# A gated cross-attention and local-attention block on one core: another table of piece times

## The chip, the core and the metric

The kernel runs on one core of one Trainium2 chip. A core has TensorE (matrix products and transposes; PE in the profile, PEld for its weight loads), VectorE (DVE), ScalarE (ACT), GpSimd (POOL) and the DMA queues, among them SP's. Each engine works through its own queue of instructions in order, and engines wait for each other by semaphores. The metric is the time of one execution on the device, in microseconds, lower is better; it is a median over runs.

## The reference

Eight sequences of 256 positions and 128 features go through a gated cross-attention (16 heads of 8) to a context of the same size, and then through six layers. Each layer is a local attention (16 heads of 64, windows of 32 that also see the window before) and a feed-forward with GELU. Half of the features are shifted by one position ahead of each. All is float32.

```python
x = x + tanh(g_xattn[0]) * xattn(layernorm(x), ctx, ctx, Wq, bq, Wk, bk, Wv, bv, Wo, bo)
x = x + tanh(g_ffn[0]) * ffn(layernorm(x), Wqkv, q_scale, k_scale, Wo, ln_g, ln_b, W1, b1, W2, b2)

# ffn: for each of 6 layers
x = attn_layer(shift_tokens(x), Wqkv[i], q_scale[i], k_scale[i], Wo[i]) + x
x = ffn_layer(shift_tokens(x), ln_g[i], ln_b[i], W1[i], b1[i], W2[i], b2[i]) + x

# attn_layer: q, k, v = split(x @ Wqkv); q, k = l2norm(q) * qs, l2norm(k) * ksc
#   rotary embedding with a scale; softmax of 8 * q k^T in windows, masked; times v; @ Wo
# ffn_layer: xn = norm(x) * g + bln; a, gate = split(xn @ W1 + b1); (a * gelu(gate)) @ W2 + b2
```

## The kernel before

A unit of work is one sequence in one layer, so there are 48 of them (`sequence(k, l, b, ...)`, k = 8 l + b), and eight cross-attentions ahead (`cross(b)`). Each is cut into named pieces; a piece is a function that issues a few instructions to one engine. For a unit the pieces are, in the order of the data:

- `proj`cx (TensorE, L537): projection of chunk c, half x, full width 128 x 128, 512 columns. Chunks 0 to 3 are keys and queries of the first 128 positions, then of the second. `sq`cx (ScalarE, L545) squares it, `rot`cx (VectorE, L553) multiplies it by the rotary tables, `ss`c (VectorE, L562) sums the squares, `radd`c (GpSimd, L568) adds the rotated halves.
- `norms` (ScalarE), `ninv` (VectorE, L584), `nrm`c (GpSimd, L591): the norms, applied. `pqt`c (TensorE, L601): transposes of 64 x 128; `qe`cx (ScalarE, L609) copies them out of PSUM. `vp`tx and `ve`tx: the values, like a projection (L616, L624).
- `sc`ti (TensorE, L637): scores of position tile t, head group i, small products of 64 x 32. `mx`gi (VectorE, L653): mask and maximum; `ex`gi (ScalarE, L663): exponentials; `rs`g (VectorE, L672), `div`g (GpSimd, L678).
- `pt`t (TensorE, L696): transposes of the probabilities, 32 x 64 and 32 x 128; `pe`tx (L705, L707) copies them out, on VectorE but for `pe00` on ScalarE; `co` (VectorE, L713) adds a corner.
- `at`c and `aw`c (TensorE, L734): attention times values in 64 x 64 pieces, in two phases, with `av`c (VectorE, L745) between; `oe`c (ScalarE, L748); `wo`x (TensorE, L757): the output projection; `oadd` (VectorE).
- `ftr` (TensorE, L770), `fst` (VectorE, L187 to L190), `frs` (GpSimd, L194), `fno` (VectorE, L198), `fba` (TensorE, L786), `faf` (VectorE, L791), `fga` and `fva` (TensorE, L806), `fge` (ScalarE, L813), `fgt` (VectorE, L819), `fdo` (TensorE, L830), `fad` (VectorE): the feed-forward.

A float32 product is two passes, and each pass is a weight load and a matmul; a transpose is one pass. So `sc`, `pt` have 128 TensorE instructions each, `at` and `aw` 64, `pqt` 32, `wo` 16, `fga`, `fva`, `fdo` 12, and `proj`, `vp`, `ftr`, `fba` 4.

The order is written out by hand. `PLAN` gives each piece a time in slots, a unit begins every 5 slots, and all pieces of all units are issued in the order of these times; only the order counts:

```python
    def at(k, piece, fn, *args):
        time = PLAN[piece] if isinstance(piece, str) else piece
        pieces.append((k * SLOTS + time, len(pieces), fn, args))
    ...
    with tc.manual_schedule():
        for _, _, fn, args in sorted(pieces, key=lambda p: p[:2]):
            fn(*args)
```

The times run to 22 slots, so at any moment four or five units are under way. `CROSS_SHIFT` moves the cross-attentions, and `LOAD_...` the weight loads on SP.

PSUM is held in three pools of two banks or bank pairs, which new tiles take in turn; a tile waits until the one two before it in its pool has been read. `ps_p` holds `proj`, `vp` and `ftr` (tags `pj`, `pv`, `px`), `ps_s` bank pairs for `pqt`, `sc` (both halves of a t in one tile), `pt`, `at` and `fga`, and `ps_m` single banks for `pt` (two), `wo`, `fba`, `fva` and `fdo`:

```python
    ps_p = ctx.enter_context(tc.tile_pool(name="ps_p", bufs=2, space=PSUM))
    ps_s = ctx.enter_context(tc.tile_pool(name="ps_s", bufs=2, space=PSUM))
    ps_m = ctx.enter_context(tc.tile_pool(name="ps_m", bufs=2, space=PSUM))
```

Of the kernel before, what the change touches and what calls it, by code (L numbers as in the profile page):

```python
# [34 lines left out]


PLAN = {
    "proj01": 0.00028, "sq01": 0.24563, "rot01": 0.27022, "proj00": 0.28172, "sq00": 0.47163,
    "rot00": 0.62148, "proj11": 0.99963, "ss0": 1.00345, "sq11": 1.0853, "rot11": 1.30237,
    "proj10": 1.30872, "sq10": 1.4114, "rot10": 1.47598, "ss1": 1.73479, "proj21": 2.11884,  # L40
    "radd1": 2.17109, "proj20": 2.19741, "sq21": 2.23333, "sq20": 2.26223, "rot21": 2.32903,
    "rot20": 2.35456, "ss2": 2.50695, "proj31": 2.58908, "radd2": 2.94111, "sq31": 2.95069,
    "rot31": 3.0918, "radd0": 3.47769, "proj30": 4.10239, "sq30": 4.10778, "rot30": 4.76634,
    "ss3": 4.85725, "norms": 5.18912, "radd3": 5.5946, "ninv": 5.62034, "nrm1": 5.71832,
    "nrm2": 6.19927, "pqt2": 6.5031, "vp00": 6.57359, "ve00": 6.87853, "nrm0": 7.09745,
    "nrm3": 7.10145, "qe21": 7.17779, "qe20": 7.24908, "pqt1": 7.30269, "pqt0": 7.30815,
    "qe11": 7.79232, "qe10": 7.79416, "qe01": 7.86086, "qe00": 7.86486, "sc01": 8.08564,
    "sc00": 8.08586, "mx01": 8.33529, "mx00": 8.575, "mx10": 8.73408, "ex01": 8.84437,
    "mx11": 9.0029, "pqt3": 9.30081, "qe30": 9.30558, "vp11": 9.34495, "qe31": 9.3858,
    "ve11": 9.41571, "ex00": 10.61127, "sc10": 10.70937, "sc11": 10.76862, "mx20": 11.07451,  # L50
    "mx30": 11.14518, "mx21": 11.1494, "ex10": 11.20658, "ex11": 11.25952, "mx31": 11.27208,
    "rs1": 11.44471, "ex30": 12.07331, "rs0": 12.16906, "ex31": 12.50422, "rs3": 12.72523,
    "div1": 12.89348, "div0": 12.89748, "pt0": 12.97352, "ex20": 13.08661, "pe01": 13.22005,
    "vp10": 13.2685, "pe00": 13.59856, "ex21": 13.65127, "ve10": 13.68936, "div3": 13.87906,
    "rs2": 14.07853, "div2": 14.3002, "pe02": 14.40755, "pt1": 14.70408, "co": 14.83618,
    "vp01": 14.9316, "pe12": 15.00601, "ve01": 15.15777, "pe11": 15.19144, "pe10": 15.19544,
    "at0": 15.39314, "av0": 15.52724, "aw0": 15.8366, "oe0": 15.91741, "at1": 16.24107,
    "av1": 16.25403, "aw1": 16.39146, "oe1": 16.45257, "wo0": 16.74993, "wo1": 17.29053,
    "oadd": 17.36809, "ftr": 17.79008, "fst": 17.79331, "frs": 17.9642, "fno": 18.23053,
    "fba": 18.70684, "faf": 19.0069, "fga": 19.48595, "fge": 19.57067, "fva": 20.02293,  # L60
    "fgt": 20.20234, "fdo": 21.23637, "fad": 21.58213, "zt": 21.88299, "zg": 21.95977,
    "xld": -23.23124, "xst": -22.91456, "xrs": -21.60601, "xno": -21.52631, "xt": -20.76317,
    "xte": -20.68889, "xqk": -19.98066, "xqe": -19.80688, "xke": -19.77245, "xb": -19.4014,
    "xs2": -18.39415, "xm22": -18.25296, "xm21": -18.24521, "xm20": -18.09159, "xvp": -18.05114,
    "xs1": -17.99064, "xve": -17.92105, "xm11": -17.83494, "xm12": -17.81429, "xm10": -17.72349,
    "xs0": -17.53644, "xm01": -17.50591, "xm02": -17.49705, "xm00": -17.31438, "xs3": -17.29615,
    "xm30": -16.85925, "xm31": -16.81729, "xm32": -16.77595, "xnt": -16.75807, "xnc": -16.74335,
    "xp1": -16.63391, "xe12": -16.58507, "xe11": -16.55896, "xe10": -16.41137, "xp0": -16.31426,
    "xa1": -16.29716, "xe02": -16.16779, "xe01": -16.16379, "xe00": -15.89622, "xo1": -15.86388,
    "xp3": -15.86254, "xa0": -15.77129, "xe31": -15.69042, "xe32": -15.66181, "xo0": -15.58029,  # L70
    "xe30": -15.44397, "xp2": -15.24929, "xa3": -15.19602, "xo3": -15.12433, "xe21": -15.10125,
    "xe22": -15.01431, "xe20": -14.75037, "xa2": -14.54131, "xo2": -14.30214, "xu0": -14.06924,
    "xd0": -14.0369, "xu1": -13.82959, "xd1": -13.5642, "xw": -13.34873, "xc": -13.29663,
    "xwo": -13.24607, "xx": -13.03102, "xst2": -12.64937, "xr2": -12.31015, "xn2": -11.66727,
    "xt2": -11.54082, "xsp": -11.45376,
}

CROSS_SHIFT = [0.0000000, -1.4843600, -2.9659400, -4.3950700, -5.7931900, -7.2641000, -8.5043100, -8.5733000]
LOAD_FIRST, LOAD_AFTER, LOAD_AFTER_CROSS = -19.7106000, 21.63, -19.98

P_ON_SCALAR = {(0, 0)}

# [2 lines left out]
def tile_gated_block(ctx: ExitStack, tc: tile.TileContext, a: dict, out: bass.AP):  # L85
# [117 lines left out]
    def cross(b):  # L203
# [203 lines left out]

        kx = b + CROSS_SHIFT[b] / SLOTS
        for n, fn in (
# [584 lines left out]
```

## Time and profile before

| | us |
|---|---|
| median of 3 runs (1817.76 to 1828.15) | 1821.45 |
| the profiled execution | 1818.11 |
| its span, first to last instruction | 1816.3 |
| busy: TensorE, VectorE, ScalarE, GpSimd | 1710.5, 1520.0, 1496.5, 1094.1 |
| first 166.8 us (cross-attention, no unit begun): TensorE busy | 149.7 |
| 460.1 to 1702.4 (units 8 to 46): TensorE busy of 1242.3 | 1202.0 |
| from the first projection of the last unit to the end | 113.9 |
| mean granted TensorE clock | 0.988 |

In a profile line of instruction groups the columns are the line of the kernel, the engine, the operation, the tiles (out<-in), the shapes and the count, then busy time and the mean duration of one in ns, and the idle time of the engine ahead of them with who ended it. "issue" as a releaser is time in which the engine waited for nothing that the profile shows. Matmuls are pipelined, so successive durations overlap; what a piece adds is the time from the end of the piece before it to its own end.

### The profile page before, as it was taken

The numbers are of one execution on the slowest core, as the hardware profiler recorded it, in microseconds if no ns is written. First come the engines' busy times: TensorE is split into PE (matmuls) and PEld (weight loads), VectorE is DVE, ScalarE is ACT, GpSimd is POOL, SyncE is SP. The second block draws the span as 40 slices with busy tenths as digits, with TensorE's granted clock in tenths as the row PEclk, the third lists the DMA queues.
The fourth block names the chain that finished last, engine by engine and source line by source line (L and its number), as shares of the span: only waits on it lengthen the run. The fifth ranks groups of instructions, "written<-read, shape, count | busy, mean of one in ns | idle before, by whom it ended". The sixth has DMA issues, their size and how long they took to land.

```text
span 1816.3 us, 78103 instructions
## 1 busy us (share of the span) xinstructions
PE 1710.5 (94%) x32948; PEld 1136.4 (63%) x32948; DVE 1520.0 (84%) x5314; ACT 1496.5 (82%) x4692; POOL 1094.1 (60%) x716
## 2 busy tenths in 40 slices
PE   7998888999999999999999999999999999999987
PEld 4565545666666666666666666666666666666664
DVE  3546667998988988899899989999899999998864
ACT  2343558998998988899989999999999999988883
POOL 3121346667676666766767676676767676766641
PEclk9999999999999999999999999999999999999998
DMA  3000002000010000010000010000100000000000
GB/s 94 7 13 11 3 2 68 3 4 3 3 48 22 3 3 3 3 49 22 3 3 3 22 49 3 3 3 3 49 22 3 3 3 4 3 6 6 8 7 10
DMA packets 34717, 26.33 MB, mean 14 GB/s; under 512 B 16058, under 2 KB 31294, under 8 KB 34366
## 3 DMA queue, kind: packets, MB, share of 16 engines
q1 hardware_dynamic: 33214, 21.20, 4.0%
q8 instruction: 259, 4.24, 1.0%
q14 instruction: 92, 0.75, 0.1%
q10 hardware_dynamic: 1152, 0.14, 0.0%
HBM read 20.28 MB, written 1.05 MB: 12 GB/s over the span
## 4 chain that ended last, share of the span: by engine, by line
PE 83%; DVE 9%; issue 5%; ACT 3%; POOL 0%; POOLq 0%; DVEq 0%; ACTq 0%
PE pj L537 18%; PE pv L616 11%; PE m L757 8%; PE po L734 8%; PE s L637 7%; PE pqt L601 6%; PE ppt L696 5%; PE s L806 5%; PE pssT L322 4%; DVE x_max L302 3%; PE pw L830 3%; PE pa L806 2%; DVE ur L553 2%; PE pox L340 1%; PE pssx L292 1%
## 5 line engine op out<-in xcount | busy, mean ns | idle before, releaser
L568 POOL TENSOR_TENSOR u<-ur 128x1024 f32<-128x1024 f32 x192 | 454.0, 2366 | 137.8 <-PE pqt L601 75.9
L663 ACT ACTIVATE pr<-pr,nmax 128x64 f32<-128x64 f32 x1536 | 513.5, 340 | 2.0 <-DVE nmax L653 1.4
L591 POOL TENSOR_TENSOR u<-u,rn 128x1024 f32<-128x1024 f32 x192 | 359.3, 1902 | 243.9 <-DVE rn L584 243.9
L537 PE MATMUL pj<-w_qkv,st 128*128 128x512 f32 x768 | 404.6, 619 | 7.0 <-DVE ur L553 3.6
L553 DVE TENSOR_TENSOR ur<-pj,rotk 128x1024 f32<-128x1024 f32 x192 | 227.1, 1203 | 85.2 <-ACT sq L545 85.2
L663 ACT ACTIVATION_READ_ACCUMULATOR pr<-pr,nmax 128x1 f32 x1536 | 294.8, 192 | 0.0
L545 ACT ACTIVATE sq<-pj 128x512 f32<-128x512 f32 x384 | 227.6, 593 | 56.8 <-PE pj L537 46.6
L678 POOL TENSOR_TENSOR pr<-pr,rs 128x512 f32<-128x512 f32 x192 | 198.6, 1046 | 91.8 <-DVE rs L672 91.8
L653 DVE CUSTOM_DVE_ANT_0 pr<-s,mask 128x64 f32<-128x64 f32 x1536 | 232.6, 219 | 17.3 <-PE s L637 16.7
L553 DVE TENSOR_TENSOR ur<-pj,rotq 128x1024 f32<-128x1024 f32 x192 | 232.7, 1212 | 15.4 <-ACT sq L545 14.3
L562 DVE TENSOR_REDUCE squares<-sq 128x16 f32<-128x1024 f32 x192 | 233.5, 1216 | 2.7
L616 PE MATMUL pv<-w_qkv,st 128*128 128x512 f32 x384 | 221.5, 659 | 1.3 <-DVE ur L553 1.0
L734 PEld LDWEIGHTS po<-prT,v 64*64 64x64 f32 x6144 | 134.3, 133 | 100.8 <-DVE nmax L653 33.4
L637 PE MATMUL s<-kT,qT 64*32 64x64 f32 x12288 | 151.9, 226 | 44.5 <-issue 44.5
L757 PEld LDWEIGHTS m<-oT,w_o 128*128 128x128 f32 x768 | 145.5, 190 | 58.9 <-issue 43.5
L757 PE MATMUL m<-oT,w_o 128*128 128x256 f32 x768 | 181.9, 380 | 0.0
L537 PEld LDWEIGHTS pj<-w_qkv,st 128*128 128x128 f32 x768 | 131.3, 192 | 79.9 <-issue 39.6
L734 PE MATMUL po<-prT,v 64*64 64x96 f32 (+1 forms) x6144 | 171.5, 243 | 8.9 <-issue 6.9
L624 ACT COPY v<-pv 128x512 f32<-128x512 f32 x192 | 112.7, 587 | 68.3 <-PE pv L616 68.2
L637 PEld LDWEIGHTS s<-kT,qT 64*32 64x32 f32 x12288 | 130.2, 105 | 58.7 <-issue 50.9
L194 POOL TENSOR_TENSOR rstd<-rstd,half_neg 128x2 f32<-128x2 f32 x64 | 45.0, 703 | 200.9 <-DVE rstd L190 173.1
L601 PEld LDWEIGHTS pqt<-ident,u 64*128 64x128 f32 x3072 | 106.7, 139 | 60.2 <-ACT pr L663 28.8
(116 smaller groups left out, 2863.3 us busy)
## 6 DMA issues: line engine op xcount, KB each, us to landing
w_qkv<-in_L_ffn_Wqkv SPq DMA_DIRECT2D x18, 512.0 KB, 6.1
w_o<-in_L_ffn_Wo SPq DMA_DIRECT2D x6, 512.0 KB, 4.0
w<-in_L_ffn_W SPq DMA_DIRECT2D x6, 341.0 KB, 2.9
xin<-in_x SPq DMA_DIRECT2D x8, 128.0 KB, 3.6
cin<-in_ctx SPq DMA_DIRECT2D x8, 128.0 KB, 2.1
out<-res SPq DMA_DIRECT2D x8, 128.0 KB, 1.8
w<-in_L_ffn_W SPq DMA_DIRECT2D x12, 64.0 KB, 3.5
rotq<-in_c_cos_q SPq DMA_DIRECT2D x6, 64.0 KB, 3.4
```

What stands on the lines that cost most here:

```text
L537: nc.tensor.matmul(pj, st[b][:, t * P : (t + 1) * P], w["qkv"][:, o : o + 512], start=True, stop=True,)
L545: nc.scalar.activation(sq[:, hs, :], c_["pj", c, half], AF.Square)
L553: nc.vector.tensor_tensor(ur[:, :, half * 512 : (half + 1) * 512].rearrange("p x (h d) -> p x h d", d=DH), pj.unsqueeze(1).to_broadcast([P ...
L562: nc.vector.tensor_reduce(squares[k % 2][:, t, i, :, 0], c_.pop(("sq", c)), AX.X, ALU.add)
L568: nc.gpsimd.tensor_tensor(u.rearrange("p h (two d) -> p h two d", two=2), ur[:, 0], ur[:, 1, :, ::-1, :], ALU.add,)
L591: nc.gpsimd.tensor_tensor(u, u, rn, ALU.mult)
L616: nc.tensor.matmul(pj, st[b][:, t * P : (t + 1) * P], w["qkv"][:, o : o + 512], start=True, stop=True,)
L637: nc.tensor.matmul(pss[n * WIN : (n + 1) * WIN, par, c, :], c_["qT"][rows, c, o : o + WIN], c_["kT"][rows, c, k0 : k0 + KEYS], start=True, ...
L653: nc.vector.tensor_tensor_reduce(probabilities(t)[:, par * NPAIR + c, :], c_["pss", t][:, par, c, :], mask[:, t, :], -1.0, 3e38, ALU.add, ...
L663: nc.scalar.activation(pr[:, col, :], pr[:, col, :], AF.Exp, bias=c_.pop(("nmax", g, c)), scale=-1.0, accum_out=c_["sums", t][:, col : col ...
L734: nc.tensor.matmul(po[par * DH : (par + 1) * DH, x, i, q0:q1], v[rows, t, h * DH : (h + 1) * DH], prT[rows, column[h], 64 * half : 64 * ha ...
L757: nc.tensor.matmul(pm, weights[l]["o"][:, c, :], oT[:, c, :], start=(first and c == 4 * half), stop=(not first and c == 4 * half + 3),)
```

## The change

The table is replaced: nearly every piece has another time, the cross-attentions another spacing, and the loads another place. No piece changes its instructions or its engine.

```diff
 PLAN = {
-    "proj01": 0.00028, "sq01": 0.24563, "rot01": 0.27022, "proj00": 0.28172, "sq00": 0.47163,
...
-    "qe11": 7.79232, "qe10": 7.79416, "qe01": 7.86086, "qe00": 7.86486, "sc01": 8.08564,
-    "sc00": 8.08586, "mx01": 8.33529, "mx00": 8.575, "mx10": 8.73408, "ex01": 8.84437,
...
-    "ve11": 9.41571, "ex00": 10.61127, "sc10": 10.70937, "sc11": 10.76862, "mx20": 11.07451,
...
+    "proj01": 0.0006328, "sq01": 0.1713858, "proj00": 0.1917734, "rot01": 0.2531156,
...
+    "radd0": 1.8177464, "rot20": 2.0866573, "proj21": 2.4116597, "sq21": 2.4285819,
+    "rot21": 2.8389973, "ss2": 3.0299221, "radd2": 3.4720543, "proj31": 3.6577322,
...
+    "pqt2": 8.1557951, "qe20": 8.3157299, "qe21": 8.3161644, "sc00": 8.5039716, "mx00": 8.7122873,
+    "pqt3": 8.9079072, "qe31": 8.9144684, "sc01": 8.920431, "mx10": 9.1908941, "qe30": 9.3090241,
...
+    "ex01": 10.2226495, "ex11": 10.4676246, "ex10": 10.6814012, "sc10": 10.7294329,
+    "mx30": 10.7734771, "mx20": 10.9018842, "rs1": 10.9979902, "sc11": 11.1160587,
...
 }
-CROSS_SHIFT = [0.0000000, -1.4843600, -2.9659400, -4.3950700, -5.7931900, -7.2641000, -8.5043100, -8.5733000]
-LOAD_FIRST, LOAD_AFTER, LOAD_AFTER_CROSS = -19.7106000, 21.63, -19.98
+CROSS_SHIFT = [0.0000000, -1.8673571, -3.6163960, -4.9323222, -6.8028984, -8.5383167, -10.3450958, -11.8335433]
+LOAD_FIRST, LOAD_AFTER, LOAD_AFTER_CROSS = -17.1923263, 20.96, -18.88
```

Sorted modulo 5 slots, the tables give the order of each engine's queue in the steady state. TensorE's, over one period (pieces of four or five units):

- before: `proj01 fva proj00 at0 sc10 sc11 aw0 proj11 fdo at1 proj10 aw1 pqt2 vp00 wo0 proj21 proj20 wo1 pqt1 pqt0 proj31 ftr pt0 sc01 sc00 vp10 fba proj30 pqt3 vp11 fga pt1 vp01`
- after: `proj01 fva proj00 at0 at1 aw0 fdo proj10 aw1 sc10 proj11 wo0 sc11 pqt1 vp00 proj20 wo1 proj21 pqt0 ftr pt0 vp10 pqt2 sc00 proj31 fba pqt3 sc01 proj30 vp11 fga pt1 vp01`

VectorE's, over the same:

- before: `pe12 pe11 pe10 fgt rot01 av0 ninv rot00 ss0 mx20 mx30 mx21 av1 mx31 rot11 rs1 rot10 fad ss1 rs0 rot21 rot20 oadd ss2 rs3 fst rot31 pe01 fno mx01 mx00 mx10 mx11 faf rs2 pe02 rot30 co ss3`
- after: `pe12 pe10 pe11 fgt av0 rot01 av1 rot00 ss0 ninv mx30 mx20 fad rot10 rs1 rot11 ss1 rs0 mx31 mx21 rot20 oadd rs2 rot21 fst pe02 ss2 fno mx00 pe01 faf rot31 mx10 rs3 mx11 mx01 rot30 co ss3`

## Prediction

> **What bounds the kernel now.** I read the page first, then who waited for whom, the DMA view, the chain in order of time over one period, and last the timelines of a period in which nothing stalls. The page:
>
> ```profile
> PE 1710.5 (94%) x32948; PEld 1136.4 (63%) x32948; DVE 1520.0 (84%) x5314; ACT 1496.5 (82%) x4692; POOL 1094.1 (60%) x716
> ...
> PE 83%; DVE 9%; issue 5%; ACT 3%; POOL 0%; POOLq 0%; DVEq 0%; ACTq 0%
> ```
>
> TensorE carries the chain, and 5% of it is "issue", time in which it waited for nothing that the profile shows. The waits say where:
>
> ```profile
> PEld s L637 <- issue: 50.9, 39, 2.0
> PE s L637 <- issue: 44.5, 37, 1.8
> ```
>
> These are the score products (both rows see the same gaps), about one gap of 1.2 us in each of the 48 periods. In the chain over 900 to 906 us one stands in the middle of the scores, right behind the transposes of probabilities:
>
> ```profile
> 901.49 1.13 PE ppt L696 x49
> 902.62 0.98 PE s L637 x65
> 903.60 1.19 issue
> 904.80 0.69 PE s L637 x44
> ```
>
> The DMA view gives the cause:
>
> ```profile
> q8 instruction: 259, 4.24, 1.0%
> ```
>
> TensorE has 2 x 32948 instructions; 4.24 MB over them is 64 bytes each, and over 259 packets 16 KB, or 256 instructions a packet. In the trace's records the gaps fall on every 256th TensorE instruction, always the same place in a packet. There are 44 over 0.3 us; all such gaps add to 52.9 us (9.4 in the first eight sequences, 39.6 in the next 39, 3.9 in the last). Beside the gap above, a packet starts at 901.93, lands at 903.36, and TensorE goes on at 904.79; the next starts 1.06 later. From entering one packet to having the next is thus 1.1 + 1.1 + 1.4 = 3.6 us (medians over the gaps), and 256 instructions that take less must wait. A period has 1276 of them, 128 in each of the two transpose pieces (1.13 us) and in each of four score pieces; two score pieces back to back are 256 instructions in 1.41 us.
>
> [...]
>
> What lies under the gaps matters as much. A period with none and one with one:
>
> ```profile
> 1479.36:1510.04 30.68, 30.66 (x640) 20.44 (x639) 28.89 (x106) 28.86 (x96) 22.20 (x14) 1.00 0.01 3
> 849.28:880.95 31.67, 30.49 (x639) 20.68 (x638) 29.06 (x106) 29.15 (x95) 21.63 (x14) 1.00 0.01 3
> ```
>
> The columns after the length are PE, PEld, DVE, ACT, POOL busy. Without a gap VectorE and ScalarE are busy 28.9 of 30.7 us. Whoever takes the gap away has 1.8 us a period of slack left on two in-order queues. From the records, counted off piece by piece in table order, the waits of TensorE in that period are 0.12 us at `vp10`, 0.22 at `fba`, 0.14 at `fga`; so its work is 30.2 us.
>
> **The change, step by step.**
>
> *Gaps.* In the new order the densest 256 instructions are the last 92 of `pt0` (0.81), `vp10` (1.06), `pqt2` (0.64) and `sc00` (0.77): 3.28 us, against 3.6. At most 0.3 us is missing, and only where a packet's edge falls there. The second densest (88 of `sc00`, `proj31`, `fba`, `pqt3`, `sc01`) gets waits put into it below. I take 3 us left of 52.9, bounds 0 and 10: **-50**.
>
> *Switches of array shape.* From one period's rows:
>
> ```profile
> 1478.39 1.12 PE L616 MATMUL pv<-w_qkv,st 128*128 128x512 f32 x2
> 1479.35 1.02 PE L537 MATMUL pj<-w_qkv,st 128*128 128x512 f32 x2
> ...
> 1484.68 0.89 PE L734 MATMUL po<-prT,v 64*64 64x96 f32 x32
> 1485.50 1.12 PE L537 MATMUL pj<-w_qkv,st 128*128 128x512 f32 x2
> ```
>
> From end to end a projection takes 0.86 us behind another full-width piece (1479.51 to 1480.37) and 1.05 behind attention (1485.57 to 1486.62): a return to full width costs 0.20. Likewise a score piece takes 0.65 behind a score piece and 0.77 behind another shape, a q/k transpose 0.50 and 0.64; attention behind attention isn't in the trace, and I give it the 0.12 of scores (bounds 0 and 0.20). Before, a period has 7 returns and 3 small pieces without a switch (`sc11`, `sc00`, `pqt0`). After, 8 returns, and only `at1` and `aw0` are without. That is 0.20 + 2 x 0.12 + 0.14 - 2 x 0.12 = 0.33 us a period, x 48: **+16**.
>
> *A chain through VectorE.* PSUM tiles of a pool take turns on two banks. In the new order `proj31` comes two `pj` tiles after `ftr`, so it can't start before `fno` has read that tile; before, it was `proj30`, behind `fba`, which needs `fno` anyway. The new VectorE queue there is `rot21, fst, pe02, ss2, fno, mx00, pe01, faf, rot31, mx10, rs3, mx11, mx01`, and `rot21` waits for `proj21`, which now stands late on TensorE, just ahead of `pqt0, ftr, pt0, vp10, pqt2, sc00, proj31`. The durations:
>
> ```profile
> 1498.78 1.22 DVE L562 TENSOR_REDUCE squares<-sq 128x16 f32<-128x1024 f32 x1
> ...
> 1500.14 0.30 DVE L187 BATCH_NORM_STATS2 stats<-px 128x6 f32<-128x128 f32 x1
> ...
> 1501.17 1.23 DVE L553 TENSOR_TENSOR ur<-pj,rotq 128x1024 f32<-128x1024 f32 x1
> 1502.31 0.68 DVE L705 COPY prT<-ppt 128x512 f32<-128x512 f32 x1
> 1502.91 0.72 DVE L198 TENSOR_SCALAR xn<-px,mv,rstd 128x128 f32<-128x128 f32 x2
> ```
>
> From end to end: `ss` 1.20, `fst` 1.09, `rot` 1.14, `pe` 0.59, `fno` 0.64; `faf` 0.46, four maxima 0.58, `rs` 0.11. Count from the end of `proj21`. `sq21` is done at 0.53, then 0.10 to VectorE, `rot21` 1.77, `fst` 2.86, `pe02` 3.45, `ss2` 4.65, `fno` 5.30; with 0.12 to restart (as behind `vp10`'s wait) `proj31` starts at 5.42. TensorE is there at 0.64 + 0.42 + 1.13 + 1.06 + 0.64 + 0.77 = 4.66: **wait 0.76**. `fba`'s bank is that which `pe01` empties: 5.30 + 0.58 + 0.59 = 6.47, and 0.32 to restart without a switch (as at `fga` now), against the end of `proj31` at 6.48: **wait 0.31**, `fba` ends at 7.01. Then `faf` 7.51, `rot31` 8.65, `mx10, rs3, mx11, mx01` 10.50. `fga` takes the bank pair of the scores `sc00` and `sc01`, freed by `mx01`: start at 10.82. TensorE gets there at 7.01 + 0.64 + 0.77 + 1.06 + 0.86 = 10.34: **wait 0.48**. Together 1.55 us a period, where 0.48 was. The waits stand behind each other on one chain, so they add; nothing covers them, since behind `proj31` TensorE's whole queue waits, and sq31, faf and the maxima behind that. 1.07 x 46 periods: **+48** (the first two run with the cross-attention). Bounds: waits of 1.0 if VectorE's steps come out a tenth shorter, 2.0 if a tenth longer, so +24 to +70.
>
> *What else moves, taken at nothing.* `frs` on GpSimd now stands behind four normalizations, one rotary addition and two divisions, 4 x 1.86 + 2.32 + 2.0 = 11.8 us after `ninv`; it starts within some 0.3 us of the end of `fst`, 0.7 us ahead of need, covered by `pe02` and `ss2`. `sc10` needs the bank that `oe0` empties on ScalarE: about 0.3 us of margin, behind which `proj11` and all else waits; a ScalarE later by 0.5 costs 0.2 x 46 = 9. `aw0` waits for `av0`, with `at1` (0.69) between: covered; without it 0.2. VectorE's `av0` comes right behind `fgt` and holds `rot01` for the end of `at0`; VectorE has slack there. The weight loads on SP move 4 us; they come over 100 us ahead of use. The cross-attention keeps its instructions at another spacing: in the first 460 us TensorE is busy 413, so 47 idle us, 9 of them gaps; I take no change and keep 10 either way. The last pieces stand 0.6 of a slot later: +1.
>
> Sum: -50 + 16 + 48 + 1 = **+15 us**. The profiled execution took 1818.1 (span 1816.3 and 1.8 around it), so 1833; the median of the three runs is 1821.45, 0.18% above it: **1836 us**.
>
> **Rivals.** (1) *The VectorE chain is shorter than its rows*, and the gaps go for little: faster. With waits as today the sum is -50 + 16 = -34 us, 1787. Break-even is a wait of 0.48 + 34/46 = 1.2 us a period; against 1.55 it takes 0.3 us off a chain of 10.5. For it: `ss` behind `rot` is 1.12, not 1.22, and two of the restarts may overlap. Against: in a period without gaps TensorE waits today at `fba` and `fga` for the same chain, with VectorE busy 94%. (2) *The chain is longer*: ScalarE holds up `sc10` or GpSimd `frs`; another 0.2 to 0.6 us, 1845 to 1866. (3) *The gaps stay*, because something other than the packets makes them, and the change doesn't do what it is built to do: 16 + 48 + 1 = +65, 1886. Gaps always on the 256th instruction speak against it. [...]
>
> **How the numbers follow.** About 0.5% (9 us) is what a measurement of this kernel can tell from no change. Forecast with waits of 1.45 to 1.9: 1831 to 1852, chance 0.46. Rival 2 0.13, rival 3 0.02: slower 0.61. Waits of 1.05 to 1.45, within 0.5%: 0.22. Rival 1 proper, below 1.05: 0.17. The range leaves out rival 3, the upper end of 2 and the lower half of 1: 1800 to 1866.
>
> **What would show it.** Right: "issue" ahead of the scores falls from 44.5 us to under 10; `proj31` idles for VectorE's `fno` some 0.7 us a period and `fga` 0.5 for the maxima; a period is about 32.1 us; a projection behind scores still ends 1.05 later. Wrong: periods under 31.3 with no VectorE wait on L537 or L806, or gaps that remain.

## Result, and the profile after

| | before | after |
|---|---|---|
| median, us | 1824.80 (1817.76 to 1828.75, 4 runs) | 1791.85 (1788.33 to 1794.04, 4 runs) |
| the profiled execution; its span | 1818.11; 1816.3 | 1788.33; 1786.5 |
| gaps at the edges of instruction packets | 52.9 | 3.7 |
| TensorE busy in units 8 to 46 | 1202.0 of 1242.3 | 39 periods, 31.16 of 31.36 each |

The changed kernel is 1.6% faster: 0.9836 of the time before (95% interval 0.9804 to 0.9867). Of the 29.8 us by which the span is shorter, 18.6 lie in units 8 to 46, 4.7 ahead of them and 6.5 behind. The forecast was 1836, 44 us too much and on the wrong side.

The page of after, busy times first, then who carries the chain:

```profile
PE 1724.5 (97%) x32948; PEld 1135.2 (64%) x32948; DVE 1558.6 (87%) x5314; ACT 1487.5 (83%) x4692; POOL 1092.7 (61%) x716
...
PE 74%; DVE 17%; ACT 4%; issue 3%; POOL 0%; DMA 0%; POOLq 0%; ACTq 0%; DVEq 0%
```

VectorE's part of the chain has doubled (9% to 17%), so the chain that I forecast through it is there. VectorE is also busy 38.6 us longer, though it executes the same 5314 instructions. From who waited for whom, in after (us in total, times, longest):

```profile
PE s L644 <- issue: 3.6, 4, 1.2
...
PE pxt L793 <- DVE xn L205: 10.1, 41, 2.5
PEld pv L623 <- DVE ur L560: 34.1, 45, 0.8
```

The gaps ahead of the scores have gone (44.5 to 3.6). What waits for VectorE now is `fba` (tile `pxt`) for `fno` and `vp11` for `rot31`, and no projection. One period of after, in the columns used before:

```profile
1459.09:1490.45 31.36, 31.16 (x639) 20.67 (x638) 29.96 (x106) 28.92 (x94) 21.63 (x14) 1.00 0.01 3
```

A period is 31.36 us against the forecast 32.1, and each from unit 4 to 46 is within 0.5 of that. VectorE is busy 29.96 in it, 1.07 more than in a period of before. The chain in order of time, cut where it leaves TensorE after `proj21` and comes back:

```profile
1477.74 1.22 DVE ur L560
...
1479.82 1.02 DVE rstd L197
1480.84 0.59 DVE prT L712
1481.43 1.13 DVE squares L569
1482.56 0.33 DVE xn L205
1482.89 0.14 issue
1483.02 0.56 PE pxt L793 x2
```

This is `rot21`, `fst`, `pe02`, `ss2`, `fno` as forecast, but it ends at `fba`, not at `proj31`; and one tiny instruction of `fst` takes 1.02 us. The groups of that instruction, before and after:

```profile
L190 DVE TENSOR_SCALAR rstd<-mv 128x2 f32<-128x2 f32 x64 | 13.8, 215 | 2.2
```

```profile
L197 DVE TENSOR_SCALAR rstd<-mv 128x2 f32<-128x2 f32 x64 | 50.7, 792 | 2.2
```

Its 36.9 us are nearly all of VectorE's extra time. The timelines of GpSimd and VectorE at that place in after:

```profile
1477.04 3.77 POOL L598 TENSOR_TENSOR u<-u,rn 128x1024 f32<-128x1024 f32 x2
```

```profile
1479.82 1.02 DVE L197 TENSOR_SCALAR rstd<-mv 128x2 f32<-128x2 f32 x1
```

GpSimd's row is `nrm2` and `nrm3`; it ends at 1480.81, and `rstd` 0.03 later. Of the 50 such instructions after the first 240 us, 46 lie beside a GpSimd normalization in after: each ends 0.02 to 0.03 us behind it and takes 0.66 to 1.31 us, according to how early it began. The other 4, and all 50 of before, have nothing of GpSimd's beside them and take 0.17.

### The profile page after: what moved, and what is told of

Same layout as the page of the kernel before. It is cut to its first block, busy times and chain, and to the rows that moved or that the text cites. A ratio compares the mean times of both kernels' runs of the same rounds, so it can differ in the third digit from the quotient of the medians.

```text
span 1786.5 us, 78168 instructions
## 1 busy us (share of the span) xinstructions
PE 1724.5 (97%) x32948; PEld 1135.2 (64%) x32948; DVE 1558.6 (87%) x5314; ACT 1487.5 (83%) x4692; POOL 1092.7 (61%) x716
## 3 DMA queue, kind: packets, MB, share of 16 engines
HBM read 20.28 MB, written 1.05 MB: 12 GB/s over the span
## 4 chain that ended last, share of the span: by engine, by line
PE 74%; DVE 17%; ACT 4%; issue 3%; POOL 0%; DMA 0%; POOLq 0%; ACTq 0%; DVEq 0%
PE pj L544 17%; PE m L764 9%; PE pv L623 9%; PE po L741 8%; PE s L644 7%; PE s L813 5%; PE pw L837 4%; PE pqt L608 4%; DVE ur L560 4%; PE ppt L703 3%; PE pssT L329 3%; DVE x_max L309 3%; DVE squares L569 3%; DVE rstd L197 2%; PE pa L813 2%
## 5 line engine op out<-in xcount | busy, mean ns | idle before, releaser
L544 PE MATMUL pj<-w_qkv,st 128*128 128x512 f32 x768 | 409.4, 615 | 5.1 <-ACT x_big L355 2.2
L670 ACT ACTIVATION_READ_ACCUMULATOR pr<-pr,nmax 128x1 f32 x1536 | 299.2, 195 | 0.0
L560 DVE TENSOR_TENSOR ur<-pj,rotk 128x1024 f32<-128x1024 f32 x192 | 234.9, 1224 | 67.7 <-ACT sq L552 60.9
L623 PE MATMUL pv<-w_qkv,st 128*128 128x512 f32 x384 | 215.7, 643 | 0.0
L741 PEld LDWEIGHTS po<-prT,v 64*64 64x64 f32 x6144 | 130.4, 133 | 72.4 <-DVE ur L560 33.4
L644 PE MATMUL s<-kT,qT 64*32 64x64 f32 x12288 | 166.0, 224 | 6.6 <-issue 3.6
L608 PEld LDWEIGHTS pqt<-ident,u 64*128 64x128 f32 x3072 | 110.4, 139 | 80.2 <-issue 68.4
L644 PEld LDWEIGHTS s<-kT,qT 64*32 64x32 f32 x12288 | 134.2, 105 | 39.7 <-issue 20.4
L741 PE MATMUL po<-prT,v 64*64 64x96 f32 (+1 forms) x6144 | 149.1, 240 | 1.4 <-DVE prT L712 1.4
L608 PE MATMUL pqt<-ident,u 64*128 64x64 f32 x3072 | 136.4, 228 | 0.3 <-DVE x_max L309 0.3
```

What stands on the lines that cost most here:

```text
L544: nc.tensor.matmul(pj, st[b][:, t * P : (t + 1) * P], w["qkv"][:, o : o + 512], start=True, stop=True,)
L560: nc.vector.tensor_tensor(ur[:, :, half * 512 : (half + 1) * 512].rearrange("p x (h d) -> p x h d", d=DH), pj.unsqueeze(1).to_broadcast([P ...
L608: nc.tensor.transpose(pt[:, h, j, :], uf[rows, j * P : (j + 1) * P], ident[rows, rows])
L623: nc.tensor.matmul(pj, st[b][:, t * P : (t + 1) * P], w["qkv"][:, o : o + 512], start=True, stop=True,)
L644: nc.tensor.matmul(pss[n * WIN : (n + 1) * WIN, par, c, :], c_["qT"][rows, c, o : o + WIN], c_["kT"][rows, c, k0 : k0 + KEYS], start=True, ...
L670: nc.scalar.activation(pr[:, col, :], pr[:, col, :], AF.Exp, bias=c_.pop(("nmax", g, c)), scale=-1.0, accum_out=c_["sums", t][:, col : col ...
```

## Experiments

My theory after the comparison: (a) the gaps belong to packet edges and dense code, and taking them away is the gain; (b) `proj31` did not wait because it got another PSUM bank than I had given it; (c) `rstd` is held by GpSimd's `nrm3`. The diffs show the changed entries alone, drawn together from several lines of `PLAN`. The table has what a piece adds, from the end of the piece before it to its own (medians of units 20 to 42, us). Without a wait they are 1.05, 0.22, 0.86 and 1.29.

| kernel | `proj31` | `fba` | `vp11` | `fga` | period | ratio to before |
|---|---|---|---|---|---|---|
| after | 1.05 | 0.73 | 1.07 | 1.29 | 31.36 | 0.9836 (0.9804 to 0.9867) |
| e1 `nrm3` behind `frs` | 1.05 | 0.22 | 1.85 | 1.29 | 31.63 | 0.9888 (0.9837 to 0.9939) |
| e2 `ve10` behind `fno` | 2.59 | 0.22 | 0.86 | 1.29 | 32.17 | 1.0062 (1.0030 to 1.0093) |
| e3 both | 1.73 | 0.22 | 1.18 | 1.29 | 31.63 | 0.9904 (0.9872 to 0.9936) |
| e5 `ss2` ahead of `fst` | 1.05 | 0.22 | 1.11 | 1.29 | 30.89 | 0.9760 (0.9724 to 0.9796) |
| e8 e5, `vp11` behind `fga` | 1.05 | 0.22 | 0.86 | 1.81 | 31.16 | 0.9815 (0.9790 to 0.9840) |
| e9 `qe30`, `qe31` behind `mx01` | 1.05 | 0.72 | 1.07 | 1.29 | 31.36 | 0.9860 (0.9827 to 0.9894) |
| e10 e8, `ex30` behind `qe30` | 1.05 | 0.22 | 0.86 | 1.29 | 30.76 | 0.9701 (0.9675 to 0.9727) |

**e1: the GpSimd piece out of the way.**

```diff
-    "nrm3": 7.8157907
+    "nrm3": 8.3536
```

> The changed kernel with one piece moved: GpSimd's normalization nrm3 goes behind frs instead of ahead of it. Theory (VectorE's rstd can't run while GpSimd's normalization runs, and ends with it): with nrm3 out of the way rstd takes about 0.17 us again instead of 1.02, fno ends 0.85 earlier, fba's wait of 0.5 us and the wait of 0.2 at vp11 go, a period falls from 31.36 to about 30.65, 46 x 0.7 = 33 us: about 1759 us (1755 to 1768). Rival (rstd is slow for a reason of its own place, or TensorE's 0.8 us of waits come from something else): period and time as they are, 1790 to 1794; if GpSimd's later nrm3 delays pqt3 or the divisions, slower than that.

1802.89 us, no gain on after (the intervals of the two ratios overlap, but a period is 0.27 longer): the theory's time was missed by 44. But `rstd` fell to a mean of 214 ns and `fba`'s wait went, as it says. The loss is elsewhere. From the waits of e1:

```profile
DVE ur L560 <- POOL u L575: 46.1, 46, 1.0
...
PE pv L623 <- DVE ur L560: 32.3, 45, 0.9
```

`radd2` stood behind `nrm3` on GpSimd as well and was now late; `rot31` waits for its buffer and `vp11` for `rot31`'s bank. I had looked only at the piece that I moved past, not at what the moved piece was then in front of.

**e2 and e3: the bank of `proj31`.**

```diff
-    "ve10": 13.2291491
+    "ve10": 13.63
```

> The changed kernel with one piece moved: ScalarE's copy ve10 goes from ahead of fno to behind it, so that when proj31 asks for a bank the one released first in the order of the program is ftr's and not vp10's. Theory (a new tile takes the bank that was released first, and my forecast gave proj31 the wrong one): proj31 now waits for fno, about 1.4 us ahead of it, fba's own 0.5 goes, and the net is about 0.95 us a period, 46 x 0.95 = 44: about 1836 us (1826 to 1845). Rival (banks strictly take turns, and the place of ve10 does not matter): 1790 to 1794, with the wait still at fba.

1836.33 us, ratio 1.0062: as the theory said. In the built kernels `proj31` lies in `vp10`'s bank in after, and in that of `ftr` in e2. The traces agree: `proj31` starts 1.47 us before the end of `fno` in after and 0.05 behind it in e2 (medians). From the waits of e2:

```profile
PE pj L544 <- DVE xn L205: 64.4, 45, 1.8
```

`proj31` waits 1.54 us a period for `fno`, and `fba` no longer does.

> Both moves: nrm3 behind frs and ve10 behind fno. This is the bank and the VectorE chain as my forecast had them: fno at its forecast time, and proj31 behind fno. By the theory proj31 waits 0.65 to 0.8 us for fno and fba hardly waits; a period is 31.3 to 31.5, 1788 to 1801 us, that is 30 to 40 us above the kernel with nrm3 moved alone. If the wait at proj31 costs nothing, it comes out as that kernel, about 1759.

1803.72 us, 31.63 a period: 2.7 us above the range, and level with e1, not 30 to 40 above it, because e1 itself had not come down. The wait itself is the forecast's: `proj31` 0.68 us late behind `fno`, where the prediction's chain through VectorE had 0.76. From the waits of e3:

```profile
PE pj L544 <- DVE xn L205: 26.5, 44, 0.8
```

**e4: packets shifted by half.** The kernel before, with 128 more TensorE instructions ahead of everything:

```diff
     for i in range(4):
         nc.tensor.transpose(pw[:, i, :], x_nat[:, i, :], ident)
+    for i in range(64):
+        nc.tensor.transpose(pw[:, i % 4, :], x_nat[:, i % 4, :], ident)
```

> The kernel before with 64 more transposes (128 TensorE instructions, half a packet) of data that is there, at the very start. Theory (gaps belong to the edges of instruction packets of 256): in the same order of pieces the gaps move: units 8 to 24 have theirs in sc01 and aw0 where they had them in sc00, and units 36 and 38 to 42, which had none, now have 1 to 1.8 us each in sc00. All gaps together stay within 45 to 62 us, time 1815 to 1835. Rival (the gaps belong to that place of the order, by data or semaphores): gaps stay in sc00 of units 8 to 30, and units 38 to 42 stay without.

1861.72 us in one run, above the range, with 76.2 us of gaps, more than the 45 to 62 expected. Their places moved as the theory says, still on every 256th instruction: `proj11` and `aw0` in units 8 to 26, where `sc00` had been; and in `sc00` 1.35 to 1.75 us in each of units 36 and 38 to 42, which had been free. From the waits of e4:

```profile
PE s L639 <- issue: 45.7, 34, 3.0
...
PE po L736 <- issue: 26.7, 17, 2.8
```

The same order of pieces thus waits at attention as well (6.9 us there before). The gaps belong to the packets and not to a place in the order. Of the 38 us above before's 1823.87 in that comparison, 23 are the larger gaps. Some of the rest is a lower clock (granted 0.978, against a median of 0.984 for the runs of before in that comparison; last section), and what then remains is open.

**e6: the changed kernel with its scores together.**

```diff
-    "sc11": 11.1160587, "sc01": 8.920431
+    "sc11": 10.74, "sc01": 8.512
```

> The changed kernel with its score pieces put back to back (sc11 right behind sc10, sc01 right behind sc00), all else in its order. Theory (256 TensorE instructions that take less than 3.6 us wait for their packet): gaps come back, from 3.7 us to 45 to 70 in all, in these four pieces and in the ones right behind them; less 0.25 us a period of saved switches and up to 0.7 of waits that they lie beside: 1815 to 1845 us. Rival (the gaps cost little, or are not made by the density of instructions): under 15 us of gaps, 1775 to 1795.

1819.27 us, ratio 1.0017 (0.9991 to 1.0042): putting the scores back together gives back the whole gain. The gaps are 29.5 us, fewer than expected:

```profile
PE s L644 <- issue: 22.8, 20, 1.6
```

The time is lost where they are. Up to the start of unit 8, with some 9 us of gaps more, this kernel falls 14.5 us behind after; in units 8 to 13, with up to two gaps a period and some 16 us in all, another 18.1; and in units 14 to 46, with next to none, it gains 2.3.

**e7: the kernel before with its scores apart.**

```diff
-    "sc11": 10.76862, "sc01": 8.08564, "sc00": 8.08586, "mx00": 8.575, "mx10": 8.73408
+    "sc11": 11.02, "sc01": 8.28, "sc00": 9.11, "mx00": 9.2, "mx10": 9.21
```

> The kernel before with its score pieces moved apart (sc11 behind proj11, sc01 behind vp10, sc00 behind proj30, with their maxima), all else in its order. Theory: gaps fall from 52.9 us to 10 to 28, about a quarter of them left where sc11 and sc10 stand close; the returns to full width and shape switches grow by some 0.65 us a period, +30 us: in sum 1805 to 1835. Rival (the gaps are not made by the density of instructions): 45 us or more of gaps stay and the switches come on top, 1845 to 1860.

The gaps fell to 1.5 us, further than expected, but the kernel took 1878.43 us, ratio 1.0340 (1.0298 to 1.0383); both forecasts of the time were wrong. From the waits of e7:

```profile
PE pv L616 <- DVE ur L553: 65.4, 47, 1.8
```

`vp10` stood behind the two score pieces and now stands ahead of them; its bank is the one that `rot31` empties, and it waits 1.4 us a period; the clock falls more often as well (15 times against 6 in units 8 to 46, last section). So spreading the scores removes gaps but is no gain by itself: the waits that a gap and 1.4 us of scores had covered come out.

**e5: another way to free `rstd`.**

```diff
-    "ss2": 3.0299221
+    "ss2": 2.87
```

> The changed kernel with one piece moved: VectorE's ss2 (1.2 us) goes ahead of fst, so that rstd comes only when GpSimd's nrm3 is done, and GpSimd's queue keeps its order. Moving nrm3 behind frs had taken the wait off rstd (0.21 us on average) and off fba, but radd2, which stood behind it, came 0.8 us later, rot31 waits for radd2's buffer, and vp11 for rot31 (0.9 us a period). Theory (rstd is held by nrm3, and it was only that delay that ate the gain): rstd 0.17 us, fno ends some 0.6 earlier, fba waits less than 0.1, rot31 hardly waits for radd2, a period is 30.65 to 30.8, 1760 to 1770 us. Rival (the waits only change place again, since VectorE's queue is as long as before between proj21 and rot31): a period stays 31.2 to 31.6, 1785 to 1803.

1770.85 us, within a microsecond of the range, period 30.89 (0.09 above it). `rstd` has a mean of 233 ns, `fba` no wait, and GpSimd's queue is untouched:

```profile
L197 DVE TENSOR_SCALAR rstd<-mv 128x2 f32<-128x2 f32 x64 | 14.9, 233 | 2.2
```

TensorE now carries nearly all of the chain:

```profile
PE 89%; DVE 5%; ACT 3%; issue 2%; POOL 0%; POOLq 0%; ACTq 0%; DVEq 0%
```

**e8 and e10: the last wait.** On top of e5, `vp11` goes behind `fga` with its copy `ve11` (e8), and then `ex30` behind `qe30` with `rs3` behind `mx11` (e10):

```diff
-    "vp11": 9.3773988, "ve11": 9.5905977, "ex30": 13.8423163, "rs3": 14.2388404
+    "vp11": 9.61, "ve11": 9.696, "ex30": 14.31, "rs3": 14.35
```

> The kernel with ss2 ahead of fst, and vp11 moved behind fga, with its copy ve11 behind fge: vp11 is what still waits in that kernel, 0.25 us a period, for rot31 to empty its bank, and fga has its input by then. Theory (that wait is all that is left between proj21 and pt1): vp11 takes 0.86 us, a period falls from 30.89 to 30.6 to 30.7, some 8 to 12 us: 1757 to 1766 us. Rival (the wait moves on, to fva or proj01 behind the later ve11 and rot30): 1768 to 1785.

1783.30 us: the rival in kind, though the wait went not to `fva` or `proj01` but to `fga`. From the waits of e8:

```profile
PEld s L813 <- ACT qT L616: 47.4, 45, 1.1
```

`fga` lies in the bank pair that `qe30` empties, and `vp11` had been its cover.

> The kernel with vp11 behind fga, where fga waited 0.52 us a period for ScalarE's copy qe30 of the bank it takes; now ScalarE's exponentials ex30 (1.33 us) go behind qe30, and VectorE's rs3 behind mx11. Theory (those exponentials were what held qe30 up): fga takes 1.29 to 1.35 us, vp11 0.86, a period is 30.6 to 30.75, 1757 to 1766 us. Rival (div3 comes too late for pt1, or sq30 for rot30, since everything on ScalarE behind ex30 moves): a period stays 30.9 to 31.3, 1770 to 1790.

1768.50 us, the fastest of all, though its interval just touches that of e5; 30.76 a period, 2.5 us above the range in time. `fga` and `vp11` wait for nothing, and 0.12 a period has moved to `fva` and `proj01`.

**e9: the bank pair of `fga`.**

```diff
-    "qe31": 8.9144684, "qe30": 9.3090241, "mx01": 9.5706932
+    "qe31": 9.4, "qe30": 9.41, "mx01": 9.35
```

> The changed kernel with ScalarE's copies qe30 and qe31 moved behind VectorE's maxima mx01, so that the score pieces' bank pair is handed back ahead of that of pqt3, and fga gets it, as my forecast had it. Theory: fga can't start before mx01 has read it, some 0.9 us after the end of vp11, that is 0.9 us a period more, 46 x 0.9 = 41: 1826 to 1840 us, with the wait at fga for VectorE's maxima. Rival (the pair makes no difference): 1788 to 1796.

1793.10 us, as after, but this tells nothing on the wait: in the built kernel `fga` still lies in `pqt3`'s pair. The place of the last reader in the program is thus not all that decides which bank is handed out; the full rule is left open.

## Why the prediction was wrong

- *Gaps, -50*: right. 52.9 to 3.7 us is -49.2, and e4 and e6 show that they are packets and density. They had a second price that I missed, in the last section: six stretches of half clock in units 8 to 46, by my estimate some 10 us at most (6 x 1.7), which the profiled execution of after does not have. The other executions of after have only a mean clock over the whole span on record (0.987 to 0.991), so what this is worth in the medians is not shown. Rival 3 falls.
- *Switches, +16*: right. The pieces without waits sum to 30.2 us a period before and 30.55 after, +0.35 where I had +0.33 (its terms add to 0.34); 48 x 0.35 = +17.
- *The VectorE chain, +48*: this step failed, at its premise "PSUM tiles of a pool take turns on two banks", which the section on the kernel before states too. In the built kernel before, the tiles at the places that I costed happen to alternate, but not all do: `vp01` takes the bank of `vp11`, the tile just ahead of it. So the premise could have been refuted before the change. After it `proj31` lies in `vp10`'s bank, already copied out; `fba` lies in the bank that `pe02` empties, not `pe01`; and `fga` in `pqt3`'s pair, not the scores'. The trace bears this out: `proj31` starts 1.47 us before `fno` ends, `fba` 1.35 before `pe01` ends, and `fga` 0.77 before `mx01` ends. So the waits at `proj31` (0.76) and at `fga` for the maxima (0.48) did not come. What came is 0.50 at `fba` for `fno` itself, 0.21 at `vp11` and 0.10 at `sc00`: 0.81 a period, not 1.55, where 0.48 was. 46 x 0.33 = +15, not +48 (46 x 1.07 is 49). `proj31`'s own 1.05 us now run beside the chain and not behind it.
- The chain as such was sized well. `fno` ended 6.12 us after `proj21`, where I had 5.30; the 0.82 between is `rstd` behind `nrm3`, which I could not read off a trace in which the two never met. With `nrm3` away, in e1 and e3, `fno` ends at 5.27; with `proj31` in the forecast bank too, e3 measures 0.68 against 0.76. And e2, with the forecast bank, takes 1836.33 us, but that agreement is luck in part: one wait of 1.54 made of the right bank and an unforeseen stall, not three of 1.55.
- *Tail, +1*, and what I took at nothing: the start of the first unit came 6.5 us earlier and the last unit's end stretch is 6.5 us shorter, but the cross-attention beside the first units gave some of that back (unit 8 starts 4.7 earlier). The start is within the 10 that I kept for it; the end is 7.5 off the forecast +1, for which I had kept nothing.

Sum of the first three with the clock at its most: -49 - 10 + 17 + 15 = -27, against -29.8 in the profiled executions; how the rest falls on the start and the end is open. The break-even that I gave for rival 1, waits of 1.2 us a period, was the right number to watch: 0.81 is below it, and rival 1 gave 1787. It won for a reason that I had not listed.

## What to carry to other kernels

Before costing a wait on a buffer, look up in the built kernel which bank each tile has: two buffers in a pool do not have to alternate (`vp01` takes the bank of `vp11` in before), and moving a reader changed the partner in e2, though not in e9. A piece that is moved in one queue moves everything behind it, so follow the next piece too (e1, e7, e8 each lost their gain to the next in line). And compare the durations of one and the same instruction in both traces first: a 0.17 us instruction that takes 1.02 stood behind most of the 0.47 us that e5 takes off a period of 31.36 by moving one neighbour.

## What the runs showed of the hardware that was not expected

**GpSimd's normalization holds up one small VectorE instruction.** `rstd` (128x2, SBUF to SBUF) ends 0.02 to 0.03 us after GpSimd's normalization where it lies beside one (46 times in after) and takes 0.66 to 1.31 us there; elsewhere it takes 0.17. The rotary product keeps its 1.2 us beside GpSimd's work in both kernels: a mean of 1.21 us in before and 1.22 in after, the same as with nothing of GpSimd's beside it. Why the one is held up and the other is not was not tested.

**The clock falls behind short idle stretches.** The granted clock falls to 0.50 in stretches of 3.413 us (each of the 6 in before); what one costs is by my estimate at most 1.7 us, half its length. In units 8 to 46 of the profiled executions before has 6, e2 7, e4 11, e6 1 and e7 15, and each begins 1.3 to 4.2 us after the start of an idle stretch of TensorE of 1.2 to 2.8 us. The kernels whose idle stretches there stay under 0.9 us (after, e1, e3, e5, e8, e9, e10) have none, though e1 has 38 of 0.6 to 0.9. The first of them in before begins at 547.6; in 6 us around it the granted clock (third column from the right) is 0.72:

```profile
546.50:552.50 6.00, 4.82 (x48) 2.60 (x48) 4.84 (x38) 3.99 (x19) 3.92 (x3) 0.72 0.01 3
```

Two periods of e7:

```profile
1561.05:1593.64 32.59, 31.06 (x639) 20.52 (x638) 29.06 (x106) 29.42 (x94) 21.67 (x14) 1.00 0.01 3
1593.64:1627.52 33.88, 32.45 (x639) 21.16 (x638) 29.05 (x106) 29.55 (x94) 21.66 (x14) 0.95 0.01 2
```

Both have the same wait; the second, at a granted clock of 0.95, is 1.29 us longer. Not each such idle stretch does it (26 over 1.0 us in before, 6 times the clock fell). Within a run the starts lie whole multiples of 3.413 us apart, as if on a grid of such steps (10, 19, 19, 10 and 56 of them in before; many in e7 are 99.0 us apart, 29 of them), and in each case of before the idle stretch begins in the step of the grid just ahead of the fall, 1.3 to 2.2 us before it. Other steps with as much idle time are not followed by a fall: in before the one with 1.24 us idle ahead of 936.7 is, and the one from 1674.0 with 1.40 is not. What sets the two apart is open.

**The fetch can start ahead of a packet.** I measured the turnaround of 3.6 us on gaps alone. In e6 two edges 1.6 us apart (in `aw1` and `sc11`) pass without a gap from the period of unit 14 on, because the fetch at the first of them starts 1.05 us ahead of that edge and not 0.78 behind it. The first edge then stands 39 instructions into `aw1` and no longer 43. That this is what moved the fetch, and why e6 has fewer gaps than expected, is argued, not shown.
